# Four fused layers on one core: WKV's transposes a step later, the last attention in two halves, and half of the weights' magnitudes on VectorE

## The chip, the cores and the metric

One core of a Trainium2 chip runs the whole program. The metric is the device time of one execution in microseconds (us), of which the median of three runs is given. Besides, one execution was taken by the hardware profiler; its busy times, waits and chains are what the sums below are made from. The engines are TensorE (PE; its weight loads, PEld, overlap its matmuls), VectorE (DVE), ScalarE (ACT), GpSimd (POOL) and SyncE (SP), which issues the DMA transfers. Each has a queue of its own and works through it in order; semaphores connect them.

## The reference

Input x has four batches of 512 tokens by 512 channels, ctx likewise. Four layers follow each other, each behind a layernorm (the last without), each added to x times tanh of a gate:

```python
x = x + tanh(g_xattn[0]) * wkv(w, u, k=layernorm(x), v=ctx)        # a scan over the tokens
x = x + tanh(g_ffn[0])   * bit_ffn(layernorm(x), w1, w2, w3)       # 512 -> 2048 -> 512
x = x + tanh(g_xattn[1]) * int8_attention(layernorm(x), ctx, ...)  # 16 heads of 32
x = x + tanh(g_ffn[1])   * ternary_linear(x, gamma, W)

# wkv: y = (A*p + E*v) / (A*q + E), with p, q, o carried from token to token
# bit_ffn: _bitlinear(x, w) = _quant_act(x) @ (sign(w) * mean(|w|)).T
h = silu(_bitlinear(x, w1)) * _bitlinear(x, w2);  out = _bitlinear(h, w3)
# attention: q = qdq(x) @ qdq(wq).T + bq; k, v from ctx; softmax; out = qdq(o) @ qdq(wp).T + bp
# ternary: xn = x * rsqrt(mean(x*x) + 1e-6) * gamma, rounded with 127 / (max|xn| + 1e-5)
```

What matters below: the FFN needs the mean magnitude of each of its three weights (1 MB pieces, four of each), the ternary layer a rsqrt and a maximum for each token, and the batches are independent of each other.

## The kernel before

**Tiles.** A batch's x lies in SBUF as `xb`, 128 tokens by 4 tiles (t) by 512 channels. WKV works on channels in four chunks (c) of 128 by 512 tokens: `chunk` (L575) makes exponentials on ScalarE, scans on VectorE (L588, L618, L623), the reciprocal of the denominator in two pieces (`wk_q`, L629), y (`wk_e`, L634), its four transposes into the PSUM tile `wy_ps` and the addition to xb (L640). The FFN works in units (t, f), f one of four slices of 2048 columns: two "up" matmul groups `ff_hp` of eight, the gate (`ff_z`, L731 to L736), a quantisation (`qg_*`, L662 to L671), transposes `tp_ps` into `hr`, and a "down" group into `ff_acc`. The attention works in units k = (pair of heads p, half h of the tokens), 16 for a batch: scores `s_ps`, their negated maximum `at_nm` on VectorE (L929), exponentials `at_P` on ScalarE (L931), transposes `pt_ps` into `at_PT` (L949, L951), values `o_ps`, and `collect`, which transposes (`ot_ps`) and divides into `at_o` (L989). Its keys, queries and values come by SyncE's DMAs from scratch memory (`fetch_keys`, `fetch_queries`, `fetch_values`, L902 to L912). Then `project_out` (L1006) rounds `at_o`, transposes (`qr_ps`), multiplies (`p_ps`), scales (`at_y`, L1022) and adds to xb (L1023, on GpSimd except in the last batch). `ternary` (L1094) normalises into `tf_xn` (L224 or L228), multiplies by gamma (L1101), takes the maximum `tf_s`, rounds (L246), transposes and multiplies (`f_ps`), and adds to xb (L1119). A rsqrt (L182) is a guess from the bits and three Newton steps on VectorE.

**Order.** The program is put together by a planner written out in the kernel. Each piece of work is a generator; `line(gen, parts)` gives its steps places on a time scale of 17 slots for a batch's FFN, and `run` always issues the step with the lowest place. What is issued first has precedence; the scheduler then fixes each engine's order. The stages are: a start (0 to about 345 us: weights' signs, magnitudes and transposes, keys and values of all contexts, WKV and FFN of batch 0, whose FFN has its weights made while it runs); a steady stage (to about 964 us: attention of batch b beside the FFN of b+1 and the WKV of b+2); and an end, in which batch 2's attention finishes, and batch 3's attention and the ternary layers run with no FFN beside them.

**PSUM.** In the start the banks are two for the tag "m" (transposes and small products), two for "hp" and four for "acc"; afterwards three, three and two. `s_ps` and `ff_hp` share "hp", `wy_ps`, `tp_ps`, `pt_ps`, `o_ps` and others share "m"; batch 3's `pt_ps` is in "acc".

**Weights at the start.** `fetch` (L303) brings 1 MB into one of two buffers `wn`; `signs` writes the signs, `magnitudes` (L327) lets ScalarE add up the absolute values in four operations. Eight pieces of the two "up" weights have to be through before the FFN's scales are known.

**Batch 3's end.** The tiles (0, 1) and then (2, 3) go through project_out and ternary (`end`, L1036), the second behind the first, while nothing else is left.

Of the kernel before, what the change touches and what calls it, by code (L numbers as in the profile page):

```python
# [10 lines left out]
F32 = mybir.dt.float32  # L11
# [19 lines left out]
def kernel(  # L31
# [150 lines left out]
    def rsqrt(v, n):  # L182
# [108 lines left out]
    class Weights:  # L291
# [35 lines left out]
        def magnitudes(self, m, f, after=None):  # L327

            wn = self.raw.pop((m, f))
            for j in range(NC):  # L330
                ins = nc.scalar.activation(
                    wn[:, j, :],
                    wn[:, j, :],
                    AF.Abs,
                    accum_out=self.asum[:, m, f, j : j + 1],
                )
                if after is not None:
                    behind(ins, after)
# [85 lines left out]
        def output_scales(self):  # L424

            pb = bank("pb_ps")
            for j in range(NC):
                full = self.pool.tile([P, P], F32, name="w_full", tag="w_full", bufs=2)
                nc.vector.tensor_copy(full, self.sp[:, j : j + 1].to_broadcast([P, P]))
                transpose(pb[:, j * P : (j + 1) * P], full, ident)  # L430
# [120 lines left out]
    def wkv_layer(b, xb):  # L551
# [23 lines left out]
        def chunk(c):  # L575
# [58 lines left out]
            nc.vector.tensor_tensor(y, A, den, ALU.mult)  # L634
            yield True
            pt = bank("wy_ps")
            for t in range(NT):
# [50 lines left out]
    def ffn_layer(xb, made=None):  # L688
# [89 lines left out]


        for n in range(len(units) + 2):  # L780
            now = n < len(units)
# [38 lines left out]
    def attention_layer(b, xb, pool, tiles=range(NT)):  # L820
# [7 lines left out]
        if b not in whole:  # L828
            whole[b] = (
                pool.tile([P, NC, T], BF16, name="at_xqT", tag="at_xqT", bufs=1),  # L830
                pool.tile([P, T], F32, name="at_sxb", tag="at_sxb", bufs=1),
                pool.tile([P, NT, D], F32, name="at_o", tag="at_o", bufs=1),
            )
        xqT, sxb, o_all = whole[b]

# [3 lines left out]
        def prepared(t, r):  # L839
# [75 lines left out]

        units = [(p, h) for p in range(NP) for h in range(len(tiles) // 2)]

# [55 lines left out]
        def collect(k):  # L973
# [4 lines left out]
            for t in range(2):  # L978
# [10 lines left out]
            nc.vector.tensor_tensor(  # L989
                o_all[:, at : at + 2, p * 64 : p * 64 + 64].rearrange(  # L990
                    "p t (i d) -> p t i d", d=DH
# [6 lines left out]
        project(0)  # L998
        fetch_keys(0)
        fetch_values(0)  # L1000
        fetch_queries(0)
        yield
        project(1)
        fetch_queries(1)
        yield
        def project_out(t):  # L1006
            s = sm.tile([P, 2], F32, name="at_s", tag="at_s")
            o = o_all[:, t, :]
            absmax(s[:, 0:1], o)
# [25 lines left out]

        def end(ts):  # L1036

            yield from together([project_out(t) for t in ts])
            r = layernorm(xb, rms=True, tiles=ts)
            yield from together([ternary(b, xb, pool, t, r) for t in ts])  # L1040


        ahead, behind_it = end((0, 1)), end((2, 3))
        ending = in_steps([ahead, behind_it], 1)

        for k in range(len(units) + 2):
# [8 lines left out]
            for i in range(2):  # L1057
                if before:
                    turned(k - 1, i, 0)
            if alone and k > len(units):  # L1060
                next_turn()
                next(ahead)
            yield
# [10 lines left out]
            if now:  # L1074
                p, h = units[k]
                if h == 0:
                    if p + 1 < NP:
                        fetch_keys(p + 1)
# [3 lines left out]
                elif p % 2 and p // 2 + 1 < NC:  # L1082
                    fetch_values(p // 2 + 1)
# [4 lines left out]
        if alone:  # L1088
            yield from ending
        else:  # L1090
            yield from in_steps([project_out(t) for t in tiles], 1)


    def ternary(b, xb, pool, t, r):  # L1094

        last = b == NB - 1
        if r is None:
            r = layernorm(xb, rms=True, tiles=[t])
        xn = pool.tile([P, D], F32, name="tf_xn", tag="at_row", bufs=ROWS)
        (centred if last else centred_aside)(xn, xb, r, t)  # L1100
        (nc.vector if last else nc.gpsimd).tensor_tensor(xn, xn, gamma_b, ALU.mult)  # L1101
        s = sm.tile([P, 3], F32, name="tf_s", tag="tf_s")
        if not last:
            yield True
        absmax(s[:, 0:1], xn)
        nc.vector.tensor_scalar(s[:, 0:1], s[:, 0:1], 1e-5, None, ALU.add)
        nc.vector.reciprocal(s[:, 1:2], s[:, 0:1])
        nc.vector.tensor_scalar(s[:, 1:2], s[:, 1:2], 127.0, None, ALU.mult)
# [3 lines left out]
        xT = pool.tile([P, NC, P], BF16, name="tf_xT", tag="at_oqT")  # L1112
        transposed_rows(xT, xn)
# [9 lines left out]
    def ternary_layer(b, xb, pool):  # L1123
        r = layernorm(xb, rms=True)
        yield from in_steps([ternary(b, xb, pool, t, r) for t in range(NT)], 1)

# [42 lines left out]
    with (  # L1169
# [19 lines left out]
        def at_unit(n):  # L1189
# [16 lines left out]
        event(at_us(31.0), lambda: context.weights_turned(1))  # L1206
        event(at_us(50.0), lambda: context.load(1))
        line(
# [5 lines left out]
            context.keys_values(1, "acc"),  # L1214
            (at_us(57.0), at_us(75.0), 4),
            (at_unit(0.5), at_unit(3.5), 4),
        )

        for m, f, fetch, use in (
# [11 lines left out]
            event(at_us(use), lambda m=m, f=f, do=do: do(m, f))  # L1231
        for m, us in ((0, 49.0), (1, 58.0)):
            line(made.turned(m, 0), (at_us(us), at_us(us + 8.0), 4))
# [54 lines left out]
    for b in range(NB):  # L1288
        if b:
# [8 lines left out]
        end = start + 18 / SLOTS  # L1298
        line(
            late(lambda b=b: attention_layer(b, xs[b], at)),  # L1300
            (b + 1.0 if b == 0 else b + 0.7, b + 1.03 if b == 0 else b + 0.9, 4),
            (b + 1 + 1.7 / SLOTS, b + 1 + 3.7 / SLOTS, 4),
            (b + 1 + 3.75 / SLOTS, b + 1 + 4.35 / SLOTS, 2),
            (start, end, 72),
            (end, end + 2.4 / SLOTS, 6),
            (end + 2.4 / SLOTS, end + 3.4 / SLOTS, 4),
        )
# [52 lines left out]
```

## Time and profile before

| | |
|---|---|
| runs | 1143.23, 1144.66, 1154.57 us (median 1144.66) |
| profiled execution | 1140.58 us, span 1138.8 us, mean clock 0.948 |
| 45 to 101 us | PE busy 41.37 of 56, DVE 37.33, ACT 37.78, clock 0.86 |
| 101 to 345 us | PE 205.18 of 244, DVE 172.50 |
| 345 to 964 us | PE 559.55 of 619, DVE 508.46, ACT 425.86 |
| 964 to 1050 us | PE 70.03 of 86, DVE 65.73, ACT 66.70 |
| 1050 to 1103 us | PE 47.84 of 53, DVE 38.90, ACT 37.00 |

The rows from the second on are busy times in windows of the trace. Of the lines quoted further on: a row of waits names the engine, its tile and line, what it waited for, then total, times and longest in us. A row of the chain of waits has start, length and what ran. "L929" is line 929 of the kernel, "x4" the number of instructions in a row. The granted clock is a share of full speed.

### The profile page before, as it was taken

To read this page: it belongs to the slowest core of one execution; us is meant where nothing else is said; L and a number is where in the kernel's file an instruction comes from. 1 tells how busy PE (TensorE), PEld (TensorE's weight loads), DVE (VectorE), ACT (ScalarE), POOL (GpSimd) and SP (SyncE) were. 2 spreads that over 40 slices of the span, in tenths; PEclk is the share of its full clock that TensorE was granted. 3 is DMA by queue.
4 is the path that set the end of the run, shared out by engine and by line. 5 is a ranking of instruction groups with operands and counts; after the bars stand their busy time and mean duration, and the time that the engine had idled before them with its cause. 6 is when DMAs were issued, how large, how long until landed. Compare 5 with 4: busy or idle time off the path is not lost.

```text
span 1138.8 us, 16572 instructions
## 1 busy us (share of the span) xinstructions
PE 967.2 (85%) x5520; PEld 679.9 (60%) x5548; DVE 877.1 (77%) x1889; ACT 722.0 (63%) x1482; POOL 320.4 (28%) x317
## 2 busy tenths in 40 slices
PE   4887898888877968889998897999999899888983
PEld 3344565555555756666776565777777677555651
DVE  5965547679878788999769899977689756688766
ACT  5777555454214576757777677687676577877763
POOL 3821014341305244441124535412122410112000
PEclk8898999999889989999998999999999999998997
DMA  8197745364425545654645544565474572333400
GB/s 277 47 299 281 282 163 184 116 236 148 148 76 192 209 166 177 186 164 169 226 173 185 169 162 137 174 217 163 176 234 149 181 232 76 105 109 103 126 5 37
DMA packets 85668, 189.58 MB, mean 166 GB/s; under 512 B 12240, under 2 KB 36816, under 8 KB 74576
## 3 DMA queue, kind: packets, MB, share of 16 engines
q1 hardware_dynamic: 85584, 188.53, 49.4%
q8 instruction: 44, 0.72, 0.3%
q14 instruction: 40, 0.33, 0.1%
HBM read 148.65 MB, written 39.85 MB: 166 GB/s over the span
## 4 chain that ended last, share of the span: by engine, by line
PE 47%; DVE 27%; ACT 15%; issue 4%; POOL 4%; DMA 2%; SPq 0%; ACTq 0%; POOLq 0%; DVEq 0%
PE ff_hp L168 13%; PE ff_acc L168 7%; PE pt_ps L171 6%; PE o_ps L168 4%; PE s_ps L168 3%; PE v_ps L168 3%; ACT at_P L931 3%; DVE at_nm L929 3%; DVE wk_q L629 3%; DVE qg_i L666 2%; PE qr_ps L171 2%; ACT wk_e L601 2%; PE tp_ps L171 2%; DVE wk_q L618 2%; ACT at_PT L951 2%
## 5 line engine op out<-in xcount | busy, mean ns | idle before, releaser
L168 PE MATMUL ff_hp<-wT,xp 128*128 128x512 f32 x1024 | 275.8, 413 | 5.9 <-ACT at_P L931 2.1
L168 PEld LDWEIGHTS ff_hp<-wT,xp 128*128 128x128 f32 x1024 | 197.0, 196 | 56.4 <-ACT at_P L931 4.6
L931 ACT ACTIVATE at_P<-s_ps,at_nm 128x512 f32<-128x512 f32 x256 | 174.6, 689 | 72.3 <-DVE at_nm L929 71.0
L929 DVE TENSOR_REDUCE at_nm<-s_ps 128x1 f32<-128x512 f32 x256 | 165.8, 678 | 28.5 <-PE s_ps L168 28.3
L671 POOL TENSOR_TENSOR ff_z<-qg_b,qg_s 128x512 f32<-128x512 bf16 x64 | 72.5, 1132 | 335.3 <-ACT qg_b L670 293.0
L951 ACT COPY at_PT<-pt_ps 128x512 f32<-128x512 f32 x224 | 124.0, 596 | 38.5 <-PE pt_ps L171 38.0
L171 PE MATMUL pt_ps<-ident,at_P 128*128 128x128 f32 x1024 | 140.9, 279 | 8.0 <-ACT at_PT L951 2.6
L168 PE MATMUL ff_acc<-wT,hr 128*128 128x512 f32 x512 | 137.9, 411 | 6.1 <-ACT hr L682 3.4
L171 PEld LDWEIGHTS pt_ps<-ident,at_P 128*128 128x128 f32 x1024 | 113.8, 141 | 48.9 <-issue 14.1
L168 PEld LDWEIGHTS ff_acc<-wT,hr 128*128 128x128 f32 x512 | 93.5, 192 | 27.0 <-ACT hr L682 4.3
L168 PE MATMUL s_ps<-at_kR,at_qR 128*128 128x512 f32 x256 | 97.6, 452 | 13.2 <-ACT at_P L931 5.4
L670 ACT CAST qg_b<-qg_i 128x512 bf16<-128x512 int8 x80 | 49.3, 617 | 59.8 <-DVE qg_i L666 53.8
L168 PE MATMUL o_ps<-at_PT,at_V 128*32 128x256 f32 x1024 | 73.0, 399 | 1.8 <-ACT at_PT L951 1.2
L731 ACT ACTIVATE ff_z<-ff_hp,coef 128x512 f32<-128x512 f32 x64 | 43.8, 684 | 46.4 <-PE ff_hp L168 42.9
L736 DVE SCALAR_TENSOR_TENSOR ff_z<-ff_hp,coef,ff_z 128x512 f32<-128x512 f32 x64 | 47.5, 743 | 29.4 <-PE ff_hp L168 29.1
L732 DVE SCALAR_TENSOR_TENSOR ff_z<-ff_z,ff_hp 128x512 f32<-128x512 f32 x64 | 43.6, 681 | 32.7 <-ACT ff_z L731 32.3
L168 PE MATMUL v_ps<-wkvT,cT 128*128 128x512 f32 x128 | 63.2, 642 | 4.2 <-ACT wT L316 3.2
L168 PE MATMUL k_ps<-cT,wkvT 128*128 128x512 f32 x128 | 61.1, 626 | 2.3 <-ACT wk_k L573 1.0
L168 PEld LDWEIGHTS s_ps<-at_kR,at_qR 128*128 128x128 f32 x256 | 45.5, 196 | 28.3 <-ACT at_P L931 13.1
L682 ACT CAST hr<-tp_ps 128x512 fp32r<-128x512 f32 x64 | 37.6, 587 | 35.6 <-PE tp_ps L171 35.6
L629 DVE RECIPROCAL wk_q<-wk_q 128x256 f32<-128x256 f32 x32 | 54.3, 1719 | 1.4 <-POOL wk_p L617 1.4
L171 PE MATMUL tp_ps<-ident,ff_z 128*128 128x128 f32 x256 | 39.9, 279 | 18.1 <-ACT at_PT L951 7.7
(179 smaller groups left out, 1757.3 us busy)
## 6 DMA issues: line engine op xcount, KB each, us to landing
wT<-wD SPq DMA_DIRECT2D x72, 1024.0 KB, 5.2
wn<-in_L_ffn_w_dram SPq DMA_DIRECT2D x18, 1024.0 KB, 6.2
at_kR<-kD SPq DMA_DIRECT2D x128, 128.0 KB, 2.9
at_qR<-qD SPq DMA_DIRECT2D x256, 64.0 KB, 2.2
wD<-wT SPq DMA_DIRECT2D x12, 1024.0 KB, 4.5
kD<-k_half SPq DMA_DIRECT2D x16, 512.0 KB, 3.2
qD<-at_half SPq DMA_DIRECT2D x32, 256.0 KB, 2.0
cn<-in_ctx_dram SPq DMA_DIRECT2D x8, 512.0 KB, 6.2
```

The costliest lines, as they stand in the source:

```text
L168: return in_turn(nc.tensor.matmul(*args, **kwargs))
L171: return in_turn(nc.tensor.transpose(*args))
L629: nc.vector.reciprocal(half, half)
L670: nc.scalar.copy(qb, qi)
L671: nc.gpsimd.tensor_tensor(grouped(src), grouped(qb), s.unsqueeze(2).to_broadcast([P, NG, GS]), ALU.mult)
L682: nc.scalar.copy(part[:, 0, :], pt)
L731: nc.scalar.activation(z, hp, AF.Tanh, scale=coef[:, 0:1])
L732: nc.vector.scalar_tensor_tensor(z, z, 1.0, hp, ALU.add, ALU.mult)
L736: nc.vector.scalar_tensor_tensor(z, hp, coef[:, 1:2], z, ALU.mult, ALU.mult)
L929: nc.vector.tensor_reduce(nm, sp, AX.X, ALU.max, negate=True)
L931: nc.scalar.activation(lanes[k, i, t], sp, AF.Exp, bias=nm, accum_out=sums[k][:, t, i : i + 1],)
L951: made[k] = nc.scalar.copy(dst, blocks(pt))
```

## The change

It has six parts. Lines after it stand 18 to 120 further down.

1. *WKV.* From batch 1 on, a chunk yields once more between y and its transposes, so that these are issued a step later.
2. *Magnitudes.* Three of the six pieces that need only their magnitude go to VectorE, one reduction over 128x2048 instead of four ScalarE operations. The places of four other steps of the start move: the load of context 1 (50 to 62.2), its keys and values (57–75 to 66.5–78.5), the first weights' transposes (49 to 56.5, 58 to 63).
3. *Broadcasts.* `output_scales` and the attention's `prepared` transpose a broadcast column directly; four VectorE copies (`w_full`, L429) and sixteen GpSimd operations (`at_full`, L848) go.
4. *Batch 0's FFN.* `down` is issued behind the second up group, not between the two.
5. *Last attention by halves.* Two attention lines, for the tiles (0, 1) and (2, 3), of eight units each. Keys and values are fetched for each half, the keys two units ahead; q_ps is made in eight pieces of 256 columns and not four of 512. The first half's units start while batch 2's are not done, its project_out and ternary lie between the second half's units. Batch 3's ternary multiplies by gamma before the rsqrt and applies the scale to the 128x1 maximum; the rsqrt's Newton steps are on GpSimd, beside.
6. *Batch 2's end.* project_out is spread, a step a unit; the ternary layer starts later, with a step more. Its buffers come from pools that are free by then.

```diff
+    def rsqrt_aside(v, n):
+        half = sm.tile([P, n], I32, name="rs_half", tag="rs_half")
+        nc.vector.tensor_scalar(half, v.bitcast(I32), 1, None, ALU.logical_shift_right)
+        y = sm.tile([P, n], F32, name="rs_y", tag="rs_y")
+        guess = nc.vector.tensor_scalar(
+            y.bitcast(I32), half, -1.0, float(0x5F3759DF), ALU.mult, ALU.add
+        )
+        for _ in range(3):
+            t = sm.tile([P, n], F32, name="rs_t", tag="rs_t")
+            nc.gpsimd.tensor_tensor(t, v, y, ALU.mult)
+            nc.gpsimd.tensor_tensor(t, t, y, ALU.mult)
+            nc.gpsimd.tensor_scalar(t, t, -0.5, 1.5, ALU.mult, ALU.add)
+            y2 = sm.tile([P, n], F32, name="rs_y", tag="rs_y")
+            nc.gpsimd.tensor_tensor(y2, y, t, ALU.mult)
+            y = y2
+        return y, guess
...
         def magnitudes(self, m, f, after=None):
             wn = self.raw.pop((m, f))
+            if f and m < 2 and (m + f) % 2 == 0:
+                nc.vector.tensor_reduce(
+                    self.asum[:, m, f, :], wn, AX.X, ALU.add, apply_absolute_value=True
+                )
+                return
...
             yield True
+            if b:
+                yield True
             pt = bank("wy_ps")
...
             yield
-            if n > 1:
-                down(*units[n - 2])
-            yield
+            if not made:
+                if n > 1:
+                    down(*units[n - 2])
+                yield
...
+            if made:
+                yield
+                if n > 1:
+                    down(*units[n - 2])
             yield
...
-            full = row("at_full")[:, 0:P]
-            nc.gpsimd.tensor_scalar(full, ones, s[:, 0:1], None, ALU.mult)
...
-            transpose(sp, full, ident)
+            transpose(sp, s[:, 0:1].to_broadcast([P, P]), ident)
...
+    def statistics(xb, tiles):
+        n = len(tiles)
+        mv = sm.tile([P, n, 2], F32, name="mv", tag="mv")
+        for i, t in enumerate(tiles):
+            s6 = sm.tile([P, 6], F32, name="s6", tag="s6")
+            nc.vector.bn_stats(s6, xb[:, t, :])
+            nc.vector.bn_aggr(mv[:, i, :], s6)
+        v = sm.tile([P, n], F32, name="ln_v", tag="ln_v")
+        nc.vector.tensor_scalar(v, mv[:, :, 1], LN_EPS, RMS_EPS, ALU.add, ALU.mult)
+        nc.vector.tensor_tensor(v, v, mv[:, :, 1], ALU.add)
+        y, guess = rsqrt_aside(v, n)
...
+        if last:
+            behind(
+                nc.vector.scalar_tensor_tensor(
+                    xn, xb[:, t, :], r[t][0], gamma_b, ALU.add, ALU.mult
+                ),
+                r[t][1],
+            )
+            absmax(s[:, 0:1], xn)
+            nc.vector.tensor_scalar(s[:, 0:1], s[:, 0:1], scale[t], 1e-5, ALU.mult, ALU.add)
...
     def ternary_layer(b, xb, pool):
         r = layernorm(xb, rms=True)
+        if b == NB - 2:
+            yield
         yield from in_steps([ternary(b, xb, pool, t, r) for t in range(NT)], 1)
...
-                (end + (3 if b < NB - 2 else 4.5) / SLOTS, end + (8 if b < NB - 2 else 12) / SLOTS, 7),
-                aside=True,
+                (
+                    (end + 3 / SLOTS, end + 8 / SLOTS, 7)
+                    if b < NB - 2
+                    else (end + 5.85 / SLOTS, end + 13.85 / SLOTS, 8)
+                ),
+                aside=b < NB - 2,
...
+        for h in range(2):
+            n = 8 * h + 0.001 * h
...
+            line(
+                late(lambda b=b, h=h: attention_layer(b, xs[b], at, range(2 * h, 2 * h + 2))),
+                rows,
+                queries,
+                (on(n - 2.15 + h * 0.95), on(n - 0.19), 1),
+                (on(n - 0.19), on(n - 0.19), 1),
+                (on(n), on(n + 10), 40),
+                *(
+                    ((on(n + 9.8), on(n + 12.8), 6),)
+                    if h
+                    else ((on(9.8), on(12.8), 3), (on(14.1), on(14.1), 1), (on(15.9), on(17.9), 2))
+                ),
             )
```

More of the change, by code (lines that the diff above doesn't have):

```diff
@@ L427, in output_scales @@
             for j in range(NC):
-                full = self.pool.tile([P, P], F32, name="w_full", tag="w_full", bufs=2)
-                nc.vector.tensor_copy(full, self.sp[:, j : j + 1].to_broadcast([P, P]))
-                transpose(pb[:, j * P : (j + 1) * P], full, ident)
+                transpose(
+                    pb[:, j * P : (j + 1) * P],
+                    self.sp[:, j : j + 1].to_broadcast([P, P]),
+                    ident,
+                )
             nc.vector.tensor_scalar(swp_b, pb, gates[:, 1:2], None, ALU.mult)
@@ L831, in attention_layer, with o_all @@
                 pool.tile([P, T], F32, name="at_sxb", tag="at_sxb", bufs=1),
-                pool.tile([P, NT, D], F32, name="at_o", tag="at_o", bufs=1),
             )
-        xqT, sxb, o_all = whole[b]
+        xqT, sxb = whole[b]
+        def o_all():
+            if (b, "o") not in whole:
+                if alone:
+                    o = ring.tile([P, NT, D], F32, name="at_o", tag="w")
+                else:
+                    o = pool.tile([P, NT, D], F32, name="at_o", tag="at_o", bufs=1)
+                whole[b, "o"] = o
+            return whole[b, "o"]
         def row(name, dtype=F32):
@@ L914, in fetch_values @@
             nc.sync.dma_start(out=V[g], in_=vD[b][:, :, g * P : (g + 1) * P])
-        units = [(p, h) for p in range(NP) for h in range(len(tiles) // 2)]
+        halves = len(tiles) // 2
+        ahead = 3 - halves
+        units = [(p, h) for p in range(NP) for h in range(halves)]
         def scores(k, i, t):
@@ L989, in collect @@
             nc.vector.tensor_tensor(
-                o_all[:, at : at + 2, p * 64 : p * 64 + 64].rearrange(
+                o_all()[:, at : at + 2, p * 64 : p * 64 + 64].rearrange(
                     "p t (i d) -> p t i d", d=DH
@@ L998, in attention_layer @@
         project(0)
-        fetch_keys(0)
-        fetch_values(0)
-        fetch_queries(0)
+        if not alone:
+            fetch_keys(0)
+            fetch_values(0)
+            fetch_queries(0)
         yield
         project(1)
-        fetch_queries(1)
+        if not alone:
+            fetch_queries(1)
         yield
+        if alone:
+            fetch_keys(0)
+            fetch_queries(0)
+            yield
+            fetch_keys(1)
+            fetch_values(0)
+            fetch_queries(1)
+            yield
         def project_out(t):
             s = sm.tile([P, 2], F32, name="at_s", tag="at_s")
-            o = o_all[:, t, :]
+            o = o_all()[:, t, :]
             absmax(s[:, 0:1], o)
@@ L1034, in together, with end @@
                 yield True
-        def end(ts):
+        def end():
+            ts = tiles
             yield from together([project_out(t) for t in ts])
[L1039 to L1044, printed above, removed]
+            means, scale = statistics(xb, ts)
+            yield from together([ternary(b, xb, pool, t, means, scale) for t in ts])
         for k in range(len(units) + 2):
@@ L1059, in attention_layer @@
                     turned(k - 1, i, 0)
-            if alone and k > len(units):
-                next_turn()
-                next(ahead)
             yield
@@ L1076, in attention_layer @@
                 if h == 0:
-                    if p + 1 < NP:
-                        fetch_keys(p + 1)
+                    if p + ahead < NP:
+                        fetch_keys(p + ahead)
                     if p % 2 == 0 and p // 2 + 2 < NC:
@@ L1081, in attention_layer @@
                         project(p // 2 + 2)
-                elif p % 2 and p // 2 + 1 < NC:
+                if h == halves - 1 and p % 2 and p // 2 + 1 < NC:
                     fetch_values(p // 2 + 1)
@@ L1088, in attention_layer @@
         if alone:
-            yield from ending
+            yield from end()
         else:
             yield from in_steps([project_out(t) for t in tiles], 1)
-    def ternary(b, xb, pool, t, r):
-        last = b == NB - 1
[L1097 to L1101, printed above, removed]
-        s = sm.tile([P, 3], F32, name="tf_s", tag="tf_s")
-        if not last:
+    def statistics(xb, tiles):
[9 more added lines that the diff above has]
+        y, guess = rsqrt_aside(v, n)
+        m = sm.tile([P, n], F32, name="ln_m", tag="ln_m")
+        nc.vector.tensor_scalar(m, mv[:, :, 0], -1.0, None, ALU.mult)
+        at = {t: slice(i, i + 1) for i, t in enumerate(tiles)}
+        return {t: (m[:, at[t]], guess) for t in tiles}, {t: y[:, at[t]] for t in tiles}
@@ new lines, in ternary @@
+    def ternary(b, xb, pool, t, r, scale=None):
+        last = b == NB - 1
+        free = b > NB - 3
+        if free:
+            xn = ff.tile([P, D], F32, name="tf_xn", tag="ff_a", bufs=3)
+        else:
+            xn = pool.tile([P, D], F32, name="tf_xn", tag="at_row", bufs=ROWS)
+        s = sm.tile([P, 3], F32, name="tf_s", tag="tf_s")
+        if last:
[4 more added lines that the diff above has]
+                r[t][1],
+            )
+            absmax(s[:, 0:1], xn)
+            nc.vector.tensor_scalar(s[:, 0:1], s[:, 0:1], scale[t], 1e-5, ALU.mult, ALU.add)
+        else:
+            centred_aside(xn, xb, r, t)
+            nc.gpsimd.tensor_tensor(xn, xn, gamma_b, ALU.mult)
@@ L1104, in ternary @@
             yield True
-        absmax(s[:, 0:1], xn)
-        nc.vector.tensor_scalar(s[:, 0:1], s[:, 0:1], 1e-5, None, ALU.add)
+            absmax(s[:, 0:1], xn)
+            nc.vector.tensor_scalar(s[:, 0:1], s[:, 0:1], 1e-5, None, ALU.add)
         nc.vector.reciprocal(s[:, 1:2], s[:, 0:1])
-        nc.vector.tensor_scalar(s[:, 1:2], s[:, 1:2], 127.0, None, ALU.mult)
+        if last:
+            nc.vector.tensor_scalar(
+                s[:, 1:2], s[:, 1:2], scale[t], 127.0, ALU.mult, ALU.mult
+            )
+        else:
+            nc.vector.tensor_scalar(s[:, 1:2], s[:, 1:2], 127.0, None, ALU.mult)
@@ L1111, in ternary @@
         yield True
-        xT = pool.tile([P, NC, P], BF16, name="tf_xT", tag="at_oqT")
+        if free:
+            xT = ring.tile([P, NC, P], BF16, name="tf_xT", tag="w")
+        else:
+            xT = pool.tile([P, NC, P], BF16, name="tf_xT", tag="at_oqT")
         transposed_rows(xT, xn)
@@ L1124, in ternary_layer @@
         r = layernorm(xb, rms=True)
+        if b == NB - 2:
+            yield
         yield from in_steps([ternary(b, xb, pool, t, r) for t in range(NT)], 1)
@@ L1206 @@
         event(at_us(31.0), lambda: context.weights_turned(1))
-        event(at_us(50.0), lambda: context.load(1))
+        event(at_us(62.2), lambda: context.load(1))
         line(
@@ L1214 @@
             context.keys_values(1, "acc"),
-            (at_us(57.0), at_us(75.0), 4),
+            (at_us(66.5), at_us(78.5), 4),
             (at_unit(0.5), at_unit(3.5), 4),
@@ L1231 @@
             event(at_us(use), lambda m=m, f=f, do=do: do(m, f))
-        for m, us in ((0, 49.0), (1, 58.0)):
+        for m, us in ((0, 56.5), (1, 63.0)):
             line(made.turned(m, 0), (at_us(us), at_us(us + 8.0), 4))
@@ L1298 @@
         end = start + 18 / SLOTS
[L1299 to L1307, printed above, removed]
         if b < NB - 1:
             line(
-                late(lambda b=b: ternary_layer(b, xs[b], at)),
-                (end + (3 if b < NB - 2 else 4.5) / SLOTS, end + (8 if b < NB - 2 else 12) / SLOTS, 7),
-                aside=True,
+                late(lambda b=b: attention_layer(b, xs[b], at)),
@@ new lines @@
+                (b + 1.0 if b == 0 else b + 0.7, b + 1.03 if b == 0 else b + 0.9, 4),
+                (b + 1 + 1.7 / SLOTS, b + 1 + 3.7 / SLOTS, 4),
+                (b + 1 + 3.75 / SLOTS, b + 1 + 4.35 / SLOTS, 2),
+                (start, end, 72),
+                (
+                    (end, end + 2.4 / SLOTS, 6)
+                    if b < NB - 2
+                    else (end - 0.15 / SLOTS, end + 5.85 / SLOTS, 6)
+                ),
+            )
+            line(
+                late(lambda b=b: ternary_layer(b, xs[b], at)),
+                (
+                    (end + 3 / SLOTS, end + 8 / SLOTS, 7)
+                    if b < NB - 2
+                    else (end + 5.85 / SLOTS, end + 13.85 / SLOTS, 8)
+                ),
+                aside=b < NB - 2,
+            )
@@ new lines, with on @@
+            continue
+        def on(n):
+            return b + 1 + (3.951 + n) / SLOTS
+        for h in range(2):
+            n = 8 * h + 0.001 * h
+            rows, queries = (
+                ((b + 0.7, b + 0.9, 4), (b + 15.8 / SLOTS, b + 17.8 / SLOTS, 2)),
+                ((on(-1.2), on(2.8), 4), (on(3.3), on(6.5), 2)),
+            )[h]
+            line(
+                late(lambda b=b, h=h: attention_layer(b, xs[b], at, range(2 * h, 2 * h + 2))),
[8 more added lines that the diff above has]
+                    else ((on(9.8), on(12.8), 3), (on(14.1), on(14.1), 1), (on(15.9), on(17.9), 2))
+                ),
```

## The prediction

> **What bounds the kernel now.** I read the page's busy shares first, then TensorE's waits, then the chain of waits in the four places that the change touches. The profiled execution has a span of 1138.8 us and took 1140.58; the median of the three runs is 1144.66. Sums are made against the first; the forecast adds their 4.1 us again.
>
> ```profile
> PE 967.2 (85%) x5520; PEld 679.9 (60%) x5548; DVE 877.1 (77%) x1889; ACT 722.0 (63%) x1482; POOL 320.4 (28%) x317
> PEclk8898999999889989999998999999999999998997
> ```
>
> TensorE does the bounding, with 171.6 us idle in all, and the clock row dips at the start and the end. So a change can only fill idle TensorE time, or move work. The waits say who causes it:
>
> ```profile
> PE qr_ps L171 <- ACT tf_xn L246: 17.6, 4, 8.0
> PE wy_ps L171 <- ACT hr L682: 11.7, 4, 3.1
> PE pb_ps L171 <- DVE w_full L429: 4.7, 2, 4.4
> PE s_ps L168 <- DMA at_qR<-qD: 4.5, 3, 3.0
> PE wy_ps L171 <- DVE wk_e L634: 4.1, 1, 4.1
> ```
>
> The first is the end, the second and fifth WKV, the fourth the seam before the last attention. Of the tail, the window row is
>
> ```profile
> 1103.00:1139.00 36.00, 15.41 (x62) 8.05 (x64) 23.76 (x84) 14.29 (x20) 0.00 (x0) 0.78 0.08 30
> ```
>
> (length, then busy PE, PEld, DVE, ACT, POOL, clock): 15.4 of 36 us of TensorE, at clock 0.78.
>
> **Tail: the last attention by halves.** The last at_o ends at 1103.08 and the last xb at 1135.30: 32.2 us for four tiles, in two rounds, each with a rsqrt chain of some 13 VectorE operations at 0.195 us. Afterwards two tiles are left. From their rows: two at_s reductions and four small operations 1.45, at_o rounding 0.82, qr_ps 0.67, its copy 0.70, p_ps 1.0; then on VectorE two at_y 1.46, two xb adds 1.2, two bn_stats 1.2, aggregate 0.2, five small ones 0.9; then rsqrt on GpSimd beside 2.6 us of VectorE (multiplying, absmax); six small ones 0.45, rounding 0.82, qr_ps and copy 1.8, f_ps of both tiles 3.1, last xb 0.75; hand-overs about 1.2. Without the rsqrt that is 17.7 us. GpSimd's twelve 128x2 operations have no row: the nearest by size is the memset of 128x1, 0.10 us; by kind the tensor_scalar of 128x128, 0.61. So 1.2 to 7.3 us; I take 0.3 each, 3.6, between the two because size should count for something. The longer of this and 2.6 counts, so the tail is 21.3 (20.3 to 25.0): **−10.9 (−7.2 to −11.9)**.
>
> [...]
>
> **What half 0 now costs beside half 1.** Its two tiles need 2 × (0.66 + 1.03 + 0.66 + 1.03) = 6.8 us of TensorE. The units there are TensorE's: 1050 to 1103 has 47.84 of 53 us busy, and a unit takes 5.3 to 5.8 us for 5.4 of matmuls. So no cover: **+7.3**, with 0.5 for q_ps in eight pieces instead of four. The extra key and value fetches (eight and four more) cost SyncE about 1.7 us of issue each time and land in 2.9; they are issued one to two units (5 to 11 us) ahead, so nothing, and 2.9 each if a unit catches up. In VectorE's new order 6.0 us (two at_y, two xb, two bn_stats, b=2's xb, small ones) stand between p_ps and the next at_nm, and TensorE has 5.5 us of matmuls until it needs the at_P behind (1.3): stall 1.8. Later a tf_s waits for GpSimd's rsqrt, with 4 us of other VectorE work before it: up to 2.4 at 0.53 us an operation, and about 2 behind that. **+3 (1.8 to 6)**.
>
> **Seam.** The last attention's first queries now start while batch 2 still computes; before, the chain of waits had
>
> ```profile
> 988.04 2.04 DMA qD<-at_half
> ...
> 990.82 2.18 DMA at_qR<-qD
> ```
>
> This chain left TensorE idle 2.96 us, and afterwards o_ps took 1.94 against 1.07 and s_ps 1.22 against 0.71: **−4.5**. Batch 2's project_out, one step a unit, also removes a wait of 2.85 us (1003.5 to 1007.2, qr_ps on at_o) with some 1.6 of slow clock: **−4.5**.
>
> **Batch 2's ternary: a new wait.** Before, its rsqrt operations stood between at_nm reductions, and what was left was a 3.58 us wait with 2.0 of slow clock behind it. In the new order of VectorE's queue they are one block: at_y (0.7), the xb add on GpSimd (1.3), bn_stats and aggregate (0.8), 15 small ones (2.9), then two tf_s reductions that wait for GpSimd, whose timeline shows how long:
>
> ```profile
> 1040.13 1.52 POOL L228 TENSOR_SCALAR tf_xn<-xb,ln_r 128x512 f32<-128x512 f32 x2 [20.70 <-PE pt_ps L171]
> 1041.62 2.50 POOL L1101 TENSOR_TENSOR tf_xn<-tf_xn,gamma_b 128x512 f32<-128x512 f32 x2
> ```
>
> That is 4.0 more and 0.65 for the last reduction: 10.6 us until the next at_nm, 11.9 until its at_P is done (0.6 + 0.7). TensorE meanwhile has s_ps 0.5, o_ps 1.0, pt_ps 1.1 and one s_ps 0.2, then waits for the bank that this at_P frees: 9.1 us, and 1.7 of slow clock by the seam's row. 10.8 − 5.6 = **+5 (−5.6 if nothing stalls)**.
>
> **WKV, wy_ps a step later.** Only five of the wy_ps groups wait in steady state, 2.6 to 4.1 us, 15.8 in all. One of them, in the chain of waits:
>
> ```profile
> 441.73 1.66 DVE wk_q L629
> 443.39 0.56 DVE at_nm L929
> ...
> 443.97 1.45 ACT at_P L931 x4
> ...
> 445.93 0.63 PE wy_ps L171 x4
> ```
>
> VectorE's reciprocals (2 × 1.7) hold up at_nm too. In the new order s_ps and ff_hp come first, but they take turns in three banks, and the next s_ps needs the ones that these at_P free at 444.6 and 445.2, so they gain some 1.3 us and not 3.1, from 446.4. VectorE is busy 29.24 of 30 us from 470 to 500. I take 1.1 each: **−5.5 (0 to −15.8)**. What is late next is the at_P.
>
> **Start.** The chain of waits in the first 100 us:
>
> ```profile
> 62.90 6.23 DMA wn<-in_L_ffn_w_dram
> ...
> 80.09 8.64 DMA wn<-in_L_ffn_w_dram
> 88.81 2.56 ACT wn L331 x8
> ...
> 91.94 1.79 ACT ff_xn L224 x3
> ```
>
> Two raw buffers alternate, so a fetch waits for the magnitudes before it; ff_xn queues on ScalarE behind a tile that was late, and the first ff_hp comes at 101.06. Afterwards three of the six pure magnitude tiles are VectorE reductions (2.27 us for 128x2048, as w_am shows, against 2.56): one buffer's chain per engine. VectorE reaches its first tile behind V, which ended at 61.8 + 0.7 = 62.5: 2.3, then twice 6.2 + 2.3, is 81.8 against 95.9, so up to 14 us, and no more than TensorE's idle there, 14.6 of 56 us from 45 to 101. K and V work moved later still has to be done. I take half: −7 (0 to −14). The w_full copies (wait 4.7) go, and so do the sixteen at_full, whose GpSimd time (9.7) nobody on the path waits for; `down` after the second up gives hr longer (ff_acc waits 3.4 + 2.7 for it): −3 (0 to −10.8). **−10 (0 to −24.8)**.
>
> **Sum**: −10.9 + 7.3 + 3 − 4.5 − 4.5 + 5 − 5.5 − 10 = −20.1: 1120.5 profiled, **1125 us** timed.
>
> **Rivals.**
> *No change, 1143.* VectorE's queue decides: batch 2's block in full, half 0's stalls at 6, GpSimd at 0.61, nothing from WKV (29.24 of 30 us speaks for it), 3 from the start: −3 − 4.5 − 4.5 + 5 + 6 + 7.3 − 7.2 = −1. Against it: TensorE waits are only moved where at_nm is late too.
> *Slower, 1157.* VectorE works in order, and a reduction that it reaches before its megabyte has landed holds up V, xb and the layernorm behind it. Three fetches waited out whole, at 6.2 to 8.6 us, cost 19 to 26; with 22 in place of −10 the sum is +12. It takes over from 10 us lost. For it: the fetches are issued after each other's release. Against: VectorE has 37.3 of 56 us busy there, so it has slack.
> *Much faster, 1101.* The start at −17, WKV −10, seam and project_out −9, batch 2's old stall gone (−5.6), half 0 at 1.8 + 7.3, tail −11.9: −44. For it: 171.6 us of idle TensorE.
>
> **Numbers.** About 1% is what a measurement here can tell. Forecast 0.54 (own range 1112 to 1138), no change 0.22, slower 0.10, much faster 0.14. Faster by over 1% (under 1133): 0.82 × 0.54 + 0.14 + 0.02 = 0.60; slower (over 1156): half of 0.10 and 0.02 of the no-change case, 0.07; the rest 0.33. The range 1102 to 1151 leaves out half of the much faster case and the slower one.
>
> **What would show it.** Tail: from the last at_o to the last xb about 21 us, one rsqrt round. Batch 2: one TensorE wait of 8 to 10 us on at_P, VectorE idle on tf_xn. Seam: no wait on at_qR of 3 us. WKV: wy_ps waits gone, in their place s_ps on at_P. Start: first ff_hp near 94, VectorE without a wait on wn. It is wrong if VectorE idles on wn, if GpSimd's small operations exceed 0.6 us, or if the fetches of keys come late.

## The result, and the profile after

The changed kernel took 1158.09 us (median of 6, 1153.39 to 1162.81) against 1143.24 (median of 6): a ratio of 1.0116, 95% interval 1.007 to 1.0162. It is slower by 1.2%, where 1125 was forecast, and it lies outside the range. The profiled execution after is the slowest of its six and the one before a fast one, so their spans differ by 21.9 us where the medians differ by 14.9: some 7 us of the differences below are scatter.

The page of the profiled execution (span 1160.7 us) has, in the rows shown of before:

```profile
PE 980.5 (84%) x5564; PEld 693.6 (60%) x5564; DVE 886.9 (76%) x1876; ACT 710.9 (61%) x1458; POOL 315.9 (27%) x325
PEclk8889999998979999999998998999999999887897
```

TensorE has 13.3 us more to do and is idle for 180.2 us and not 171.6, and the granted clock is under 0.9 in five of the last six slices, where before it was so in two. The spans cut at four marks of the traces (the starts of the first ff_hp, the first s_ps, the last ff_acc and the last s_ps) show where:

| us | before | after | difference |
|---|---|---|---|
| start to first ff_hp | 100.1 | 99.4 | −0.7 |
| to first s_ps | 290.2 | 283.5 | −6.7 |
| to last ff_acc | 573.3 | 572.6 | −0.7 |
| to last s_ps | 130.0 | 167.2 | +37.2 |
| to the end | 45.2 | 38.0 | −7.2 |

The start gained, the tail gained, and the stretch without an FFN beside the attention lost far more than both. TensorE's waits of the whole execution:

```profile
PE s_ps L168 <- ACT at_P L976: 34.1, 22, 9.6
...
PE qr_ps L171 <- ACT tf_xn L264: 10.0, 1, 10.0
...
PE s_ps L168 <- DMA at_qR<-qD: 4.6, 3, 2.9
```

The first row was, before:

```profile
PE s_ps L168 <- ACT at_P L931: 5.4, 11, 1.2
```

The waits for pb_ps are gone from the list and those for wy_ps but for 0.7 us, that for tf_xn is one and not four, and that for at_qR is as it was. How at_P comes late is read from VectorE's timeline:

```profile
1010.81 0.75 DVE L1078 SCALAR_TENSOR_TENSOR at_y<-p_ps,at_s,swp_b 128x512 f32<-128x512 f32 x1
1012.94 0.69 DVE L225 BATCH_NORM_STATS2 s<-xb 128x6 f32<-128x512 f32 x1 [1.38 <-POOL xb L1079]
1013.67 0.18 DVE L228 BATCH_NORM_AGGREGATE mv<-s 128x2 f32<-128x6 f32 x1
1013.77 1.25 DVE L974 TENSOR_REDUCE at_nm<-s_ps 128x1 f32<-128x512 f32 x2
...
1047.64 0.15 DVE L238 SCALAR_TENSOR_TENSOR ln_r<-mv,rs_y 128x4 f32<-128x4 f32 x1
1050.78 0.69 DVE L249 TENSOR_REDUCE tf_s<-tf_xn 128x1 f32<-128x512 f32 x1 [2.98 <-POOL tf_xn L1183]
1052.00 0.69 DVE L249 TENSOR_REDUCE tf_s<-tf_xn 128x1 f32<-128x512 f32 x1 [0.54 <-POOL tf_xn L1183]
1052.60 1.28 DVE L974 TENSOR_REDUCE at_nm<-s_ps 128x1 f32<-128x512 f32 x2
```

Batch 2's project_out makes at_y, GpSimd adds it to xb, and the bn_stats of batch 2's ternary, already queued, waits for that ahead of the next at_nm. On TensorE, in its timeline, it looks so:

```profile
1015.29 0.49 PE L168 MATMUL s_ps<-at_kR,at_qR 128*128 128x512 f32 x1 [2.61 <-ACT at_P L976]
...
1026.01 0.50 PE L168 MATMUL s_ps<-at_kR,at_qR 128*128 128x512 f32 x1 [1.69 <-ACT at_P L976]
...
1036.45 0.51 PE L168 MATMUL s_ps<-at_kR,at_qR 128*128 128x512 f32 x1 [1.87 <-ACT at_P L976]
...
1054.21 0.79 PE L168 MATMUL s_ps<-at_kR,at_qR 128*128 128x512 f32 x1 [9.61 <-ACT at_P L976]
```

The last is the block that the prediction had seen (9.1 us worked out, 9.61 found). The three before it, one in each unit, it had not. From one o_ps to the next, these four units took 11.6, 10.3, 10.0 and 17.0 us. The granted clock is 0.50 behind each of the three (1017.5 to 1020.8, 1027.8 to 1031.0, 1038.0 to 1041.2) and from 1048.3, within the long wait, to 1061.7.

### The profile page after: what moved, and what is told of

It reads as the page before. It is cut to its first block, busy times and chain, and to the rows that moved or that the text cites. A ratio compares the mean times of both kernels' runs of the same rounds, so it can differ in the third digit from the quotient of the medians.

```text
span 1160.7 us, 16660 instructions
## 1 busy us (share of the span) xinstructions
PE 980.5 (84%) x5564; PEld 693.6 (60%) x5564; DVE 886.9 (76%) x1876; ACT 710.9 (61%) x1458; POOL 315.9 (27%) x325
## 4 chain that ended last, share of the span: by engine, by line
PE 48%; DVE 25%; ACT 13%; issue 5%; DMA 5%; POOL 4%; SPq 0%; POOLq 0%; ACTq 0%; DVEq 0%
PE ff_hp L168 14%; PE ff_acc L168 6%; PE pt_ps L171 6%; ACT at_P L976 3%; PE v_ps L168 3%; PE s_ps L168 3%; PE o_ps L168 3%; PE k_ps L168 3%; DVE at_nm L974 3%; DVE wk_q L655 2%; PE qr_ps L171 2%; PE tp_ps L171 2%; DMA wn<-in_L_ffn_w_dram 2%; DVE qg_i L695 2%; PE ot_ps L168 1%
## 5 line engine op out<-in xcount | busy, mean ns | idle before, releaser
L171 PE MATMUL pt_ps<-ident,at_P 128*128 128x128 f32 x1024 | 146.8, 286 | 16.7 <-ACT at_PT L996 9.6
L171 PEld LDWEIGHTS pt_ps<-ident,at_P 128*128 128x128 f32 x1024 | 118.4, 146 | 57.8 <-issue 15.6
```

Of the source, the lines that this page charges most:

```text
L171: return in_turn(nc.tensor.transpose(*args))
```

## The experiments

All are compared with the kernel before, which had medians of 1143.88 to 1145.35 beside them. First, the last stretch.

**Batch 2's end placed as before**, all else changed:

```diff
         r = layernorm(xb, rms=True)
-        if b == NB - 2:
-            yield
...
-                    else (end - 0.15 / SLOTS, end + 5.85 / SLOTS, 6)
...
+                (end, end + 2.4 / SLOTS, 6),
...
-                    else (end + 5.85 / SLOTS, end + 13.85 / SLOTS, 8)
...
-                aside=b < NB - 2,
+                (end + (3 if b < NB - 2 else 4.5) / SLOTS, end + (8 if b < NB - 2 else 12) / SLOTS, 7),
+                aside=True,
```

> The changed kernel with batch 2's project_out and ternary placed as in the kernel before (four project_out in 2.4 slots, the ternary layer in whole slots after it, no extra yield); all else changed. Theory 1 (batch 2's end, spread, puts at_y, bn_stats and rsqrt in VectorE's queue ahead of at_nm, three or four units of 10.5 us instead of 5.5 and one block of 10): the stretch from the last ff_acc to the last s_ps falls from 167 us to 140 to 147, the time by 20 to 27 us, to 1131 to 1138. Rival (the halves themselves, with their fetches, q_ps pieces and half 0's end, cost the time): less than 8 us saved, 1150 or more.

1148.43 us (1.0061, 1.0029 to 1.0093), 9.7 less than the changed kernel by the medians and 6.3 by the two ratios, with some 6 us of uncertainty: too little for theory 1 and at the upper end of the rival's. The last stretch is 156.2 us. Of the three units one is left (9.0 us, with a wait of 2.4 for at_P), but one of 16.8 us with a wait of 8.8 is there again. So the block does not come from the spreading.

**The bn_stats kept in program order**, one word, the places as changed:

```diff
-        r = layernorm(xb, rms=True)
+        r = layernorm(xb, rms=True, pinned=b == NB - 2)
```

> The changed kernel with the bn_stats of batch 2's ternary kept in program order, so that they stand behind the at_nm of the units over which project_out is spread; the rsqrt block and its wait for GpSimd stay. Theory 1, if it is the GpSimd addition and bn_stats that lengthen each unit (1.3 + 0.7 us of the 10.6 us cycle, three times): 6 to 8 us saved. Theory 1b, if at_y alone, queued before at_nm, closes the cycle: 6 to 8 saved too but units of 8.6 us remain, not 5.5. Rival (halves): under 2 us.

1144.67 us (0.9993, 0.9971 to 1.0015): 13.4 less, twice what was expected. The at_nm now come directly behind at_y:

```profile
1005.08 0.75 DVE L1078 SCALAR_TENSOR_TENSOR at_y<-p_ps,at_s,swp_b 128x512 f32<-128x512 f32 x1
1005.75 1.28 DVE L974 TENSOR_REDUCE at_nm<-s_ps 128x1 f32<-128x512 f32 x2
```

The four units take 9.6 (with a wait of 1.6 for a key fetch in it), 6.2, 6.1 and 5.9 us, and the longest wait for at_P is 2.5. The four bn_stats follow together, once all additions are done, and two at_nm stand among the first rsqrt operations, so the block is open too. Of the 21 us that the four units lose, 9 come back behind them: the next two take 10.8 and 10.5 us, where they took 6.0 and 6.8. Theory 1 holds, 1b does not: with at_y alone ahead of at_nm, units of 8.6 us do not remain.

**Both**, places as before and bn_stats in program order:

> The changed kernel with batch 2's project_out and ternary placed as before and their bn_stats kept in program order: the halves without the spreading and without the early bn_stats. Theory 2 (halves cost about 10): within 3 us of the 1144.7 that the changed kernel with pinned bn_stats took. Rival (spreading costs): 1136 or less.

1145.22 us (1.0012, 0.9992 to 1.0032), 0.6 from the version before: with the bn_stats in order, the spreading is neither gain nor loss that can be measured.

**The whole last attention**, with the parts that gained (below), batch 2's end spread and the bn_stats in program order:

> The same kernel (parts 1, 3, 4) and part 6, batch 2's project_out spread and its ternary later, with the bn_stats kept in program order; the last attention whole, in its old order. Theory 2 (beside the bn_stats it is the halves that cost, about 10 us, by their stalls and slow clock): within 4 us of the kernel without part 6. Rival (spreading itself, at_y before at_nm in each unit, costs): 8 us or more slower than that.

1129.76 us (0.9871, 0.9843 to 0.9898), 1.2 less than without the spreading (1130.93, below), which is within the noise. The version with the halves took 1144.67, so the halves and the magnitudes together cost 14.9. The windows from the last ff_acc to just behind the last s_ps, first whole, then by halves (length, busy PE, PEld, DVE, ACT, POOL, clock):

```profile
956.50:1083.70 127.20, 108.96 (x850) 73.66 (x856) 99.61 (x238) 99.31 (x244) 17.16 (x16) 0.97 0.34 102
```

```profile
949.70:1105.90 156.20, 123.83 (x878) 83.05 (x876) 111.43 (x273) 102.81 (x254) 19.91 (x28) 0.88 0.41 117
```

29 us more: 14.9 of TensorE busy (the p_ps, f_ps, qr_ps and q_ps of the first half are 7.9 of it by their groups; the others take longer at the lower clock), and 14.1 of it idle. The tail behind gives 4.3 back, and with the halves and the magnitudes the stretch begins 6.8 us earlier, so the total of 14.9 hides a part of what the stretch costs.

**The first half's end taken out of the second half's units** and put behind them:

```diff
-                    ((on(n + 9.8), on(n + 12.8), 6),)
+                    ((on(n + 11.6), on(n + 14.6), 6),)
...
-                    else ((on(9.8), on(12.8), 3), (on(14.1), on(14.1), 1), (on(15.9), on(17.9), 2))
+                    else ((on(18.0), on(19.0), 3), (on(19.1), on(19.1), 1), (on(19.2), on(19.5), 2))
```

> The changed kernel with pinned bn_stats, and the first half's project_out and ternary taken out from between the second half's units and put behind them. Theory 2a (what costs in the halves is the first half's end inside the second half's units, stalls of at_nm behind its VectorE work and the slow clock after them): the stretch from the last ff_acc to the last s_ps falls from 155 us to 135 or less, more than the 8 us of matmuls taken out; the tail grows. Rival 2b (the units of a half themselves are slower, by their fetches or their order): 145 or more.

1148.09 us (1.0024, 1.0 to 1.0048): no gain, as the tail grew. The stretch fell from 155.2 to 144.9 us, by 8.5 of busy TensorE and 1.8 of idle: no more than its matmuls and a little, so theory 2a falls. With the whole attention it is 126.2, and 18.7 of the 29 us are still there. Where the rest lies shows unit by unit (worked out from TensorE's timeline, o_ps to o_ps, around batch 2's ternary):

```
whole attention      5.8   6.2   6.8   9.6   6.2   6.5   5.8
halves (end moved)   5.9  10.4  10.9   7.5  12.3   6.4   6.5
```

The same steps of batch 2 cost one long unit with the whole attention, and three with the halves. VectorE's order differs: with the whole attention the bn_stats and the rsqrt steps are interleaved with at_nm reductions; with the halves there are four bn_stats in a row, then fifteen tf_s operations with no at_nm among them.

**The tf_s maxima in program order too**, with the halves:

```diff
-            absmax(s[:, 0:1], xn)
+            top = nc.vector.tensor_reduce(
+                s[:, 0:1], xn, AX.X, ALU.max, apply_absolute_value=True
+            )
+            if b == NB - 2:
+                tc.keep_in_program_order(top)
```

> The changed kernel with pinned bn_stats, and the tf_s maxima of batch 2's ternary kept in program order too, so that they no longer wait for GpSimd ahead of at_nm. Theory 2c (in the halves the scheduler packs batch 2's ternary into blocks on VectorE between at_nm pairs, units of 10.4, 10.9 and 12.3 us, where the whole attention has them interleaved, 6.2, 6.8 and 9.6): 3 to 6 us saved against 1144.7, since two of the three blocks shrink. Rival 2b (the halves' own order and fetches): within 1.5 us.

1141.78 us (0.9971, 0.9953 to 0.9988): 2.9 less than with the bn_stats alone in order, at the edge of theory 2c, with an uncertainty of about 3.

**Without batch 2's ternary layer**, whole and by halves:

> The kernel with parts 1, 3, 4, 6, pinned bn_stats and the last attention whole, without batch 2's ternary layer (its xb goes out as the attention leaves it). Its matmuls (6.8 us) and its VectorE blocks go: 1129.8 less 10 to 14, 1116 to 1120.

> The changed kernel with pinned bn_stats (halves), without batch 2's ternary layer likewise. With it, halves took 14.9 us more than the whole attention, of which 2 are the magnitudes' and 8 the first half's matmuls less 4 to 5 of the tail. Theory 2c (blocks of batch 2's ternary make the rest): without the layer the difference to the whole attention falls to 4 to 8 us, this kernel to 1121 to 1127. Rival 2b: it stays at 12 or more, 1129 or above.

1120.29 (1117.13 to 1126.56) and 1128.29 us (1120.61 to 1133.21). The difference falls from 14.9 to 8.0 by the medians, the upper end of theory 2c's range, and from 14 to 9 by the ratios; the second time lies above the 1121 to 1127 that the theory gave. The runs scatter by more than in the others, and the fall is not clear of that. In the profiled executions the stretch to the last s_ps is 119.1 and 138.3 us: 19.2 more by halves, where it was 29.0 with the layer. So a part of the halves' loss seems to go with that layer, a third to a half, and not more can be said.

Now the parts that gain. **WKV's yield alone** (one `yield True` for b ≥ 1):

> The kernel before with the one added yield ahead of WKV's transposes, nothing else. My forecast: 5.5 us saved (0 to 15.8). Theory now, from the changed kernel's steady stage, which is 0.7 us shorter (first s_ps to last ff_acc 572.6 against 573.3): under 2 us, since s_ps waits for at_P in its place. Rival: the full 5 us are there and another part gives them back in that stage.

1139.63 us (0.9963, 0.9946 to 0.9981): 4.4 less, nearer to the rival's 5. From 350 to 964 us its waits of TensorE begin with

```profile
PE s_ps L168 <- ACT at_P L933: 8.1, 9, 2.2
```

where before 15.8 us for wy_ps stood: the wait has changed its place and halved. But in the profiled executions the steady stage (first s_ps to last ff_acc) is only 1.3 us shorter, and the last stretch 2.2; the same two differences come again between the two versions below that differ by this yield.

**The magnitudes alone**, with the moved places of the start:

> The kernel before with part 2 alone: three magnitude tiles on VectorE and the four moved places of the start. My forecast: 7 us saved (0 to 14). Theory now, from the first ff_hp at 99.4 in the changed kernel against 100.1: under 1.5 us either way, the weights' DMA sets the FFN's start. Rival: the 7.4 us by which the first s_ps came earlier are from this part, through keys and values moved out of the way.

1146.11 us (1.0018, 1.0002 to 1.0034): 2 us slower, if anything. What sets the FFN's start is in the changed kernel's chain of waits:

```profile
87.53 0.45 PE wt_ps L171 x8
87.98 10.36 PE k_ps L168 x24
98.34 0.44 PE tp_ps L171 x4
...
100.57 1.89 PE ff_hp L168 x7
```

TensorE works through 10.4 us of key products that stand before the FFN's transposes; they are those of context 1, and part 2 itself had moved them later (the first began at 77.2 before, at 83.9 after). And the last tile reached VectorE no earlier: its fetch was issued at 84.1 us, behind a transfer that waited for ScalarE, and its reduction ran at 95.7, so that the sums were there at 98.2, when the key products ended too (98.3).

With parts 3 and 4 beside them the magnitudes look otherwise. In the profiled executions the first s_ps comes at 379.8 to 382.9 us in the seven versions that have parts 2 to 5, and at 384.0 to 389.8 in the six that have parts 3 and 4 without part 2; alone, part 2 left it at 390.2 against 390.3. No run separates part 2 from the halves there.

**Broadcasts and down alone** (parts 3 and 4 of the diff):

> The kernel before with parts 3 and 4 alone (broadcast columns transposed directly; batch 0's down behind the second up). Theory: the 7.4 us by which the changed kernel reached its first s_ps earlier are these, as magnitudes alone did not move it: first ff_hp unchanged near 100, first s_ps near 383, the time 6 to 8 us less. Rival: they come from parts 2 and 3 or 4 together, or are given back: under 3 us.

1138.47 us (0.9952, 0.9936 to 0.9968): 5.4 less, a little under the expected 6 to 8. First ff_hp at 103.3, first s_ps at 384.3: the FFN with its weights made beside it takes 281.0 us and not 290.2.

**Together with WKV's yield:**

> The kernel before with parts 1, 3 and 4 (WKV's yield, broadcasts, down), the attentions' ends and the magnitudes as before. If the savings add (4.4 measured for the yield, 6 to 8 expected of the other two): 1131 to 1134. If the earlier start is lost again in the steady stage: 1137 to 1140.

1130.93 us (0.9896, 0.9874 to 0.9918): 13 less; the two added give 9.8, and the noise allows for the rest.

Two tries to take more from the version with the whole last attention. **The new last ternary** in its tail (gamma first, scale on the maximum, rsqrt on GpSimd):

> The kernel with parts 1, 3, 4, 6 and pinned bn_stats, the last attention whole, and of part 5 only the new last ternary: gamma before the rsqrt, the scale applied to the 128x1 maximum, the Newton steps on GpSimd. My forecast for this arithmetic within the tail: GpSimd's twelve operations 3.6 us beside 2.6 of VectorE. In two rounds of two tiles each it should shorten the tail by 2 to 5 us against 1129.8 without it. Rival: GpSimd's chain is as long as VectorE's was and nothing is gained, within 1 us.

1128.8 us (0.9869, 0.9844 to 0.9893) against 0.9871: no gain that can be seen. **Its first projections two slots earlier:**

```diff
-            (b + 1 + 1.7 / SLOTS, b + 1 + 3.7 / SLOTS, 4),
-            (b + 1 + 3.75 / SLOTS, b + 1 + 4.35 / SLOTS, 2),
+            *(
+                ((b + 1 - 0.3 / SLOTS, b + 1 + 1.7 / SLOTS, 4), (b + 1 + 1.75 / SLOTS, b + 1 + 2.35 / SLOTS, 2))
+                if b == NB - 1
...
```

> The kernel with parts 1, 3, 4, 6 and pinned bn_stats, the last attention whole, its first two projections and fetches placed two slots earlier. My forecast priced the seam (a wait for at_qR of 2.96 us and slow clock behind it) at 4.5; the changed kernel left it at 2.9 us. If the wait is only a matter of place: it goes, 3 to 4.5 us saved against 1129.8. Rival (the last batch's inputs are late themselves, the projection cannot start earlier): within 1 us.

1131.77 us (0.9889, 0.9861 to 0.9917): no gain either. The wait for at_qR is gone, and its waits of TensorE from 950 to 1090 have instead

```profile
PE qr_ps L171 <- ACT at_xn L246: 4.8, 1, 4.8
```

Of the versions that beat both kernels, the four best cannot be told apart: parts 1, 3 and 4 (0.9896), with the spread end (0.9871), and this with the new last ternary (0.9869) or the early projections (0.9889).

## Why the prediction was wrong

The forecast was −20.1 and the runs show +14.9. The steps between the two: −13 (parts 1, 3 and 4), −1 (spreading with the bn_stats in order), +15 (halves and magnitudes), +13.4 (bn_stats early). These are differences of versions that follow each other, so they have to add up, but for half a us by which the kernel before varied, and check nothing; how the +15 divides between halves and magnitudes is not measured. By the prediction's steps:

- *WKV, −5.5*: −4.4. The reading that s_ps would wait for at_P in its place was right. That the size was met is in part luck: the gain was forecast for the steady stage, and in the profiles that gives 1.3, the last stretch 2.2.
- *Start, −10*: the w_full copies and `down`, sized at −3, gave −5.4 (with the sixteen at_full operations), and the wait for w_full was followed by one of 5.2 us for swp_b; so it is `down` behind the second up, it seems, though these were not run apart. The magnitudes, sized at −7, gave +2 by themselves, and the first ff_hp came at 99.4 where 94 was named. The step that failed is "no more than TensorE's idle there": I bounded the gain by TensorE's idle time and halved it, and did not ask what stands in TensorE's queue in front of the FFN.
- *Tail, −10.9*: from the last at_o to the last xb 23.3 us, forecast 21.3, before 32.2: −8.9. GpSimd's twelve operations took 4.06 us with their gaps, 3.6 was taken. The rest of the 2 us is TensorE's: qr_ps to p_ps took 3.67 us for 2.37 worked out, f_ps 3.53 for 3.1, at a granted clock of 0.64 from 1134 to 1158 us, where the tail before had 0.78.
- *Seam, −4.5*: not there, the wait is 2.9 us as before. "Start while batch 2 still computes" was true of the places, not of the chain: the projection waits for its inputs' rounding. Forcing it earlier only moved the wait, as shown.
- *project_out spread, −4.5*: this step failed, and here the cause is shown. I took the old wait away and looked for a new one only in batch 2's ternary. In the new order of VectorE's queue the bn_stats stood after each at_y, before the at_nm, and each waited for GpSimd's addition; I counted them once, in the block, and there were four units. Their price, with the block's part that went with them, is the 13.4 us of the pinned version.
- *Batch 2's ternary, +5*: the wait was 9.6 for 9.1 worked out. (The terms of the block add up to 10.35 us, not to the 10.6 written; from at_y to the next at_nm the trace has 10.7.) Right in mechanism and size, but the two gains that I set against it did not come.
- *Half 0's work, +7.3 and +3*: these two terms were met, as far as one pair of profiles shows. Taking the first half's end out of the units shortened the stretch by 10.3 us, 8.5 of it busy TensorE. (The 0.53 us an operation in the term for tf_s stands in no row; the tail's twelve took 0.34 each with their gaps.) What failed is that I put nothing else down for the halves: beside the whole attention the stretch is 29 us longer, and 18.7 of them stay without the first half's end. These 18.7 us are the largest miss of all. Of the 29 about 10 seem to go with batch 2's ternary layer, which VectorE works off in longer runs of operations between the at_nm than with the whole attention; the units and the 2.9 us of the tf_s in order support that, but do not show it. If these and the first half's end do not overlap, some 9 us stay open, with one new wait of 1.6 for a key fetch among them.

The "no change" rival had VectorE's queue as its reason, with the right place, and stopped at 1143 for want of the three units and of most of the halves' loss. The "slower" rival's 1157 lies next to the measured time by luck: it named VectorE waiting for the weights, and its waits for wn sum to 1.6 us.

## What to carry to other kernels

When a step is spread over units, look in the other engines' queues for what depends on its product and is already due: it moves with it, and stands in each unit where it waits. Here the unit closes a loop over three engines (s_ps, at_nm, at_P, bank), and what stood in VectorE's queue before at_nm lengthened it, though VectorE was busy for only 76% of the span. And where a gain is bounded by an engine's idle time, check first what that engine has queued in front of the work that is to start earlier.

## What the runs showed of the hardware

GpSimd's 128x2 operations in the tail's timeline:

```profile
1145.78 0.63 POOL L209 TENSOR_TENSOR rs_t<-ln_v,rs_y 128x2 f32<-128x2 f32 x1 [43.65 <-DVE rs_y L204]
1146.48 0.58 POOL L210 TENSOR_TENSOR rs_t<-rs_t,rs_y 128x2 f32<-128x2 f32 x1
1147.15 0.19 POOL L211 TENSOR_SCALAR rs_t<-rs_t 128x2 f32<-128x2 f32 x1
1147.43 0.20 POOL L213 TENSOR_TENSOR rs_y<-rs_y,rs_t 128x2 f32<-128x2 f32 x1
```

The first two of a chain take 0.6 us, the other ten 0.19 to 0.20, with 0.07 to 0.08 between them (from start to start 0.70 and 0.67 us, then 0.27 to 0.29); in the version with two such chains the second one's first two took 0.63 and 0.58 again, only 2.7 us after the first chain. Why is open. One of the ten is about as long as VectorE's on 128x2 in the tail before (0.16 to 0.17 us, one each 0.2). But a Newton step is four operations here, 1.10 us, and three on VectorE, 0.59; so the move to GpSimd frees VectorE and shortens nothing by itself, and the version that tried it alone was no faster.
